# Two levels of Strassen's form for the output projections of chunk 14, with the inner sums on VectorE

## The chip, the cores and the metric

The kernel runs on one core of a Trainium2 chip. The metric is the time of one execution in device microseconds (us). TensorE (PE) multiplies, and its weight loads are shown as a row of their own (PEld); VectorE (DVE), ScalarE (ACT) and GpSimd (POOL) do elementwise work; SyncE (SP) issues most DMAs. Every engine works through its own queue in program order.

## The reference, cut to what matters

All data are float32. `x` has 8 sequences of 1024 rows of 512, so 8192 rows.

```
xn = layernorm(x)
proj = xn @ W1 + b1                       # 512 -> 3 * 1024: hidden, forget, input
...                                        # gated recurrence along each sequence -> out_h
s = out_h @ W2 + b2                       # 1024 -> 512
shared = (silu(xn @ sgate) * (xn @ sup)) @ sdown        # 512 -> 1024 -> 512
routed = expert e of each row (the best of 32 by xn @ gate_w), the same form with its own weights
x = x + s * silu(shared + routed)
```

The change is in the two products with a 1024 x 512 matrix: `out_h @ W2` (called half 0 in the kernel) and the shared expert's product with `sdown` (half 1).

## The kernel before, in words

**Two stages.** In the first stage the rows are taken in 16 chunks of 512 (`NCHUNK`, `T`), numbered 0 to 15. Each chunk has its projections in (W1, sgate, sup: 20 jobs), its recurrence, and its projections out. In the second stage the 32 experts work on rows gathered by expert; its order doesn't depend on the change. A last loop for overflowing experts follows.

**The order of the first stage** is written out by hand: a loop over slots (`now`), 7 slots to a job, so 140 to a chunk (`SC`). In each slot every engine gets its next instructions: two TensorE products of a projection in (`multiply`, line 925), the steps planned for that slot (`at(slot, ...)`), and as many steps of the generator `project_out` as `due(slot)` says. The projections out of chunk c run while chunk c + 1 is projected in: half 0 over the first 62 slots, half 1 over the other 74. The projections out of chunk 15 have nothing beside them: they begin with slot 142 after the start of chunk 15, at a rate of 7/3 steps to a slot, and after them the expert stage begins.

**Projections out.** Each half of a chunk is 7 products (`UNIT`, Strassen's form of one level). A *whole* product is 8 matmuls with 256 columns (line 1461), evicted as one tile of 128 x 512 by ScalarE or VectorE (`out_copy`, lines 1325 and 1331). A *deep* product is split again into 7 inner products (`INNER`: P1, P2, P5, P6, P3, P7, P4) of 2 matmuls with 128 columns each (line 1407), one inner product to a step. In the profile each of these float32 matmuls leaves two records, so a whole product has 16 and a deep one 28. `deep(b)` says which products are deep: those of chunks 1 to 13. Chunks 0, 14 and 15 are whole.

The inner products of one deep product begin three steps apart and those of neighbouring products are interleaved: P1 at step 7b, P2 at 7b + 3, and so on to P4 at 7b + 18. So the last deep unit has 6 inner products left when its own steps are over; they are put between the matmuls of the next unit's first whole product, one for one (`left` in `project_out`).

P1, P6, P7 and P4 share one region of a PSUM bank: each is added onto the one before it, which must have been evicted first. P2, P3 and P7 are evicted by VectorE, which adds a part kept from before (line 1416), P1, P5, P6 and P4 by `out_copy`. So P4 waits for VectorE's eviction of P7, three steps ahead of it.

A deep product needs 4 sums of blocks of its left operand (`inner_sum`, line 1389): 8 instructions of 128 x 128 where the operand is a block of the activations themselves (products P1, P2, P4 of `UNIT`), else 4 of 128 x 256. GpSimd makes them. Each sum has one buffer (`i1` to `i4`).

**Weights for the projections out** come by `out_fetch` on SP's queue into a ring of 3 tiles of 512 KB: a whole product's weights by one DMA of 512 KB (`w_whole`), the weights of four inner products by four of 128 KB (`w_pieces`). A fetch is issued when the tile three back is used up. After the slot loop three more tiles (`far`) are added.

**Beside chunk 15's projections in**, GpSimd writes the table of the rows' places with 64 small indirect DMAs (line 1706, `tab`). SP reads it back (`two`), VectorE merges it, and the first expert's rows are gathered by it.

Of the kernel before, what the change touches and what calls it, by code (L numbers as in the profile page):

```python
# [34 lines left out]
def tile_kernel(  # L35
# [45 lines left out]
    nc = tc.nc  # L81
# [8 lines left out]
    NCHUNK = N // T  # L90
# [436 lines left out]
    def alloc2(shape, tag, name):  # L527
# [11 lines left out]
            lambda t, b, e=e: pools["fours"][:, b, e * CT + t : e * CT + t + 1],  # L539
# [606 lines left out]
    ALL = [(c, half, name) for c, half in units for name in UNIT]  # L1146

    def deep(b):
        return 0 < ALL[b][0] < NCHUNK - 2

    LAST = max(b for b in range(len(ALL)) if deep(b))
    inner_of = {}
    for b in range(len(ALL)):
        if deep(b):
            for i, name in enumerate(INNER):
                inner_of[7 * b + 3 * i] = (b, name)
# [4 lines left out]
    def out_order():  # L1161

        piece = []
        for b, u in enumerate(ALL):
            if deep(b):
                piece += [(7 * b + k) for k in range(7)]
                if b == LAST:
                    piece += [7 * b + k for k in range(7, 19)]
                continue
            yield from groups(piece)  # L1170
            piece = []
            yield ("whole", b)
            if u[0] == 0:
                yield ("made", b)
        yield from groups(piece)
# [84 lines left out]
    def out_part(c, half, p):  # L1260
        h = (rnn_h, ffn_h)[half][c, p]
        return [h[:, k, m * HALF : (m + 1) * HALF] for m in range(2) for k in range(2)]
# [102 lines left out]
    def inner_block(b, m, k):  # L1365

        c, half, name = ALL[b]
        part = slice(m * P, (m + 1) * P)
        if name in RAW:
            return [out_part(c, half, 2 * k + q)[RAW[name]][:, part] for q in range(2)]  # L1370
        return [out_s[(c, half), SUM[name]][:, 2 * k : 2 * k + 2, part]]

    def inner_sum(b, q):

        o = inner[b, q] = jp.tile([P, 2, P], FP, tag=f"i{q}", name=f"i{q}_{b}", bufs=1)
        A11, A12, A21, A22 = (inner_block(b, m, k) for m in range(2) for k in range(2))
        n = len(A11)
        parts = [o[:, i, :] for i in range(2)] if n == 2 else [o]

        def made(q):  # L1380
            t = inner[b, q]
            return [t[:, i, :] for i in range(2)] if n == 2 else [t]

        l, r, what = {
            1: lambda: (A21, A22, ALU.add), 2: lambda: (made(1), A11, ALU.subtract),
            3: lambda: (A11, A21, ALU.subtract), 4: lambda: (A12, made(2), ALU.subtract),
        }[q]()
        for o, l, r in zip(parts, l, r):
            nc.gpsimd.tensor_tensor(o, l, r, what)  # L1389

    def inner_lhs(b, name):
        if name in RAW:
# [33 lines left out]
    def project_out():  # L1426
# [11 lines left out]
        for b, (c, half, name) in enumerate(ALL):  # L1438
            if deep(b):
                for k in range(7):  # L1440
                    step(7 * b + k)
                    if k % 3 == 0 and k < 9:
                        inner_sum(b, (1, 2, 4)[k // 3])
                    if k == 2 and deep(b - 1):
                        inner_sum(b - 1, 3)
                    yield
                continue
# [4 lines left out]
            for q in range(2):  # L1452
                for p in range(NP):
# [27 lines left out]
                    if left and b > LAST:  # L1481
                        step(left[0])
                        if left[0] == 7 * LAST + 9:
                            inner_sum(LAST, 3)
                        left.pop(0)
                        yield
# [540 lines left out]
```

## Time and profile before

| what | us |
|---|---|
| runs of the kernel: median (lowest to highest of 3) | 4140.21 (4139.19 to 4141.18) |
| the profiled execution: its time | 4142.6 |
| its span, first to last instruction | 4140.9 |
| TensorE busy in the span | 4057.0 (98%) |
| VectorE, ScalarE, GpSimd busy | 2647.0, 2203.4, 2198.8 |
| chunk 13's projections in (out of chunk 12, deep) | 2206.6 to 2376.1 |
| chunk 14's projections in (out of chunk 13, deep) | 2376.1 to 2551.0 |
| chunk 15's projections in (out of chunk 14, whole) | 2551.0 to 2735.6 |
| the rest of the projections out of chunk 15 | to 2781.1 |
| the experts | from 2781.1 |

Each stretch of a chunk is cut so that it holds the 560 records that a chunk leaves at line 925. Line numbers (L925) are those of the kernel before. In a timeline a row holds the start, the time until its last instruction ends, the engine, line and operation, `out<-in` by tile names, and the count; in brackets the idle time before it and what ended it. In a table by stretches the columns are the stretch, its length, the busy time of PE, PEld, DVE, ACT and POOL with their counts, the granted TensorE clock, the share of the DMA engines and GB/s.

### The profile page before, as it was taken

Reading aid. Unit: us, or ns where it says so; the run is one execution under the profiler, and the core shown is the slowest. Engines: PE = TensorE matmul, PEld = TensorE weight load, DVE = VectorE, ACT = ScalarE, POOL = GpSimd, SP = SyncE. Lnnn points to the kernel's source line nnn. Section 1 sums busy time; section 2 is a strip of 40 time slices with the busy share of each in tenths; the row PEclk is TensorE's granted clock in tenths of the full one; section 3 lists DMA queues with packets and bytes.
Section 4 is the critical chain, followed back from the end, with each engine's and each line's share of the span. In section 5 each row is a group of like instructions: output and inputs, shape, how many; then the busy total and the mean of one; then the engine's idle time right before and its main releaser. Section 6 shows DMA issues by size and latency. Waiting matters only on the chain. (4 is left out here: it accounts for less than half of the span.)

```text
span 4140.9 us, 70159 instructions
## 1 busy us (share of the span) xinstructions
PE 4057.0 (98%) x23699; PEld 3642.7 (88%) x23699; DVE 2647.0 (64%) x4553; ACT 2203.4 (53%) x4582; POOL 2198.8 (53%) x2539
## 2 busy tenths in 40 slices
PE   8999999999999999999999999999999999999997
PEld 6788889888888888988988888887899999999997
DVE  6666676677766766667676677444556656666631
ACT  5777676776767667676677765731222222222210
POOL 4324565565655655556655564634555555565542
PEclk9999999999999999999999999999999999999999
DMA  8788787787877778778777776666777787888884
GB/s 285 254 285 270 236 257 250 249 259 244 260 242 242 252 254 255 249 236 258 253 249 251 237 250 205 187 214 200 211 228 229 223 245 230 244 254 234 247 259 117
DMA packets 731387, 994.43 MB, mean 240 GB/s; under 512 B 75468, under 2 KB 523884, under 8 KB 730772
## 3 DMA queue, kind: packets, MB, share of 16 engines
q1 hardware_dynamic: 682020, 896.52, 68.0%
q0 software_dynamic: 46880, 89.20, 8.7%
q8 instruction: 193, 3.16, 0.3%
q10 hardware_dynamic: 2128, 4.19, 0.3%
q14 instruction: 166, 1.36, 0.1%
HBM read 858.39 MB, written 149.21 MB: 243 GB/s over the span
## 5 line engine op out<-in xcount | busy, mean ns | idle before, releaser
L925 PE MATMUL b<-t,sums 128*128 128x256 f32 x2536 | 652.7, 380 | 11.0 <-ACT u L939 5.2
L339 PE MATMUL acc<-e_h,e_wd 128*128 128x284 f32 (+26 forms) x2048 | 514.7, 394 | 0.0
L925 PEld LDWEIGHTS b<-t,sums 128*128 128x128 f32 x2536 | 454.2, 191 | 61.7 <-ACT u L939 7.3
L1407 PEld LDWEIGHTS u<-w_pieces,i 128*128 128x128 f32 x2912 | 435.4, 191 | 73.2 <-POOL i L1389 31.5
L1407 PE MATMUL u<-w_pieces,i 128*128 128x128 f32 x2912 | 445.4, 275 | 22.4 <-POOL i L1389 16.1
L339 PEld LDWEIGHTS acc<-e_h,e_wd 128*128 128x128 f32 x2048 | 373.6, 190 | 64.9
L260 POOL DMA_INDIRECT e_xs<-rec,fours x276 | 301.2, 1091 | 91.3 <-issue 88.6
L925 PE MATMUL b<-t,nat 128*128 128x256 f32 x1268 | 327.2, 381 | 5.3 <-ACT u L939 3.7
L925 PE MATMUL c<-xnT,sums 128*128 128x256 f32 x1268 | 326.8, 380 | 2.8 <-ACT p L939 2.8
L925 PE MATMUL c<-t,sums 128*128 128x256 f32 x1268 | 328.0, 381 | 0.1
L925 PE MATMUL b<-xnT,nat 128*128 128x256 f32 x1268 | 327.7, 381 | 0.0
L925 PE MATMUL a<-xnT,nat 128*128 128x256 f32 x1268 | 326.0, 380 | 0.2 <-ACT c L939 0.2
L302 POOL COPY pin<-e_h 1x1 f32<-1x1 f32 x148 | 37.7, 255 | 477.1 <-DVE e_h L447 348.3
L1389 POOL TENSOR_TENSOR i<-s 128x256 f32<-128x256 f32 x208 | 222.5, 1072 | 99.5 <-PE u L1407 75.8
L941 ACT ACTIVATE u<-b,vec 128x256 f32<-128x256 f32 x378 | 180.9, 478 | 175.3 <-PE b L925 168.8
L925 PEld LDWEIGHTS b<-xnT,nat 128*128 128x128 f32 x1268 | 226.2, 191 | 35.4 <-DMA w_pieces<-d_P 6.7
L925 PEld LDWEIGHTS b<-t,nat 128*128 128x128 f32 x1268 | 227.4, 191 | 32.2 <-ACT u L939 5.0
L925 PEld LDWEIGHTS c<-xnT,sums 128*128 128x128 f32 x1268 | 226.1, 191 | 28.8 <-ACT p L939 6.0
L925 PEld LDWEIGHTS c<-t,sums 128*128 128x128 f32 x1268 | 225.6, 191 | 27.6 <-DVE lgT L694 5.3
L925 PEld LDWEIGHTS a<-xnT,nat 128*128 128x128 f32 x1268 | 226.0, 191 | 23.2 <-ACT c L939 0.6
L414 ACT COPY e_s<-e_b 128x284 f32<-128x284 f32 (+21 forms) x216 | 84.4, 391 | 239.2 <-PE e_b L405 239.2
L1407 PEld LDWEIGHTS u<-w_pieces,s 128*128 128x128 f32 x1248 | 187.6, 191 | 26.3 <-DVE o L1416 10.2
(328 smaller groups left out, 9523.5 us busy)
## 6 DMA issues: line engine op xcount, KB each, us to landing
w_pieces<-d_P SPq DMA_DIRECT2D x1274, 128.0 KB
sums<-sdram SPq DMA_DIRECT2D x300, 512.0 KB
nat<-in_L_attn_W_dram SPq DMA_DIRECT2D x192, 512.0 KB
e_w<-L_ffn_routed_gate_w_dram SPq DMA_DIRECT2D x126, 512.0 KB
e_w<-n_L_ffn_routed_up_w_dram SPq DMA_DIRECT2D x126, 512.0 KB
e_wd<-L_ffn_routed_down_w_dram SPq DMA_DIRECT2D x31, 2048.0 KB
nat<-L_ffn_shared_gate_w_dram SPq DMA_DIRECT2D x64, 512.0 KB
nat<-n_L_ffn_shared_up_w_dram SPq DMA_DIRECT2D x64, 512.0 KB
```

What stands on the lines that cost most here:

```text
L260: nc.gpsimd.indirect_dma_start(out=self.xs[t][:, b, :], out_offset=None, in_=rec1.rearrange("n (a d) -> (n a) d", a=NA), in_offset=bass.In ...
L302: nc.gpsimd.tensor_copy(pin, self.mark)
L339: nc.tensor.matmul(accs[m][:, :W], lhsT=self.wd[:, j, m * P : (m + 1) * P], rhs=h[:, :W], start=(j == 0), stop=(j == NI - 1),)
L414: nc.scalar.copy(o[:, :W], ps[:, :W])
L925: nc.tensor.matmul(ps, lhsT=lhs[:, k, :], rhs=rhs[:, k, :], start=(new and k == 0), stop=(k == KQ - 1),  skip_group_check=True,)
L941: nc.scalar.activation(o, ps, AF.Identity, bias=bias(n, block))
L1389: nc.gpsimd.tensor_tensor(o, l, r, what)
L1407: nc.tensor.matmul(ps, lhsT=lhs, rhs=w[:, i, :], start=(name == "P1" and i == 0), stop=(i == 1), skip_group_check=True,)
```

## The change

Chunk 14's 14 products become deep, and `inner_sum` uses VectorE for them. Chunks 1 to 13 keep theirs on GpSimd. Everything else follows from `deep(b)`: `PER` gives each half of chunk 14 49 steps instead of 56, the 6 inner products left over by chunk 13 go on among chunk 14's deep steps, and 6 of chunk 14's now stand among the first matmuls of chunk 15's output.

```
     def deep(b):
-        return 0 < ALL[b][0] < NCHUNK - 2
+        return 0 < ALL[b][0] < NCHUNK - 1
...
     def inner_sum(b, q):
 
         o = inner[b, q] = jp.tile([P, 2, P], FP, tag=f"i{q}", name=f"i{q}_{b}", bufs=1)
+        eng = nc.vector if ALL[b][0] == NCHUNK - 2 else nc.gpsimd
         A11, A12, A21, A22 = (inner_block(b, m, k) for m in range(2) for k in range(2))
...
         for o, l, r in zip(parts, l, r):
-            nc.gpsimd.tensor_tensor(o, l, r, what)
+            eng.tensor_tensor(o, l, r, what)
```

More of the change, by code (lines that the diff above doesn't have):

```diff
@@ L1148, in deep @@
     def deep(b):
-        return 0 < ALL[b][0] < NCHUNK - 2
+        return 0 < ALL[b][0] < NCHUNK - 1
     LAST = max(b for b in range(len(ALL)) if deep(b))
@@ L1375, in inner_sum @@
         o = inner[b, q] = jp.tile([P, 2, P], FP, tag=f"i{q}", name=f"i{q}_{b}", bufs=1)
+        eng = nc.vector if ALL[b][0] == NCHUNK - 2 else nc.gpsimd
         A11, A12, A21, A22 = (inner_block(b, m, k) for m in range(2) for k in range(2))
@@ L1388, in inner_sum @@
         for o, l, r in zip(parts, l, r):
-            nc.gpsimd.tensor_tensor(o, l, r, what)
+            eng.tensor_tensor(o, l, r, what)
     def inner_lhs(b, name):
```

## The prediction

> **What bounds the kernel now.** First the page's busy times.
>
> ```profile
> span 4140.9 us, 70159 instructions
> PE 4057.0 (98%) x23699; PEld 3642.7 (88%) x23699; DVE 2647.0 (64%) x4553; ACT 2203.4 (53%) x4582; POOL 2198.8 (53%) x2539
> ```
>
> TensorE is the bound: what counts is the time that its matmuls take in its queue, and the places where it waits. Next the stretches of a deep chunk (out of chunk 12) and of the one that changes (out of chunk 14).
>
> ```profile
> 2206.60:2376.10 169.50, 167.62 (x966) 150.15 (x966) 118.42 (x193) 118.84 (x242) 96.83 (x117) 1.00 0.78 249
> 2551.00:2735.60 184.60, 179.82 (x836) 157.65 (x835) 97.92 (x144) 116.97 (x212) 107.48 (x104) 0.99 0.59 182
> ```
>
> The second is longer, with VectorE and the DMA engines less busy. What a matmul costs, and the one long wait, stand in TensorE's timeline there.
>
> ```profile
> 2554.44 0.61 PE L1407 MATMUL u<-w_pieces,i 128*128 128x128 f32 x4
> 2554.88 1.03 PE L925 MATMUL c<-xnT,sums 128*128 128x256 f32 x4
> 2555.75 0.59 PE L1461 MATMUL u<-w_whole,h 128*128 128x256 f32 x2
> 2556.18 1.03 PE L925 MATMUL b<-xnT,nat 128*128 128x256 f32 x4
> 2560.89 0.71 PE L1407 MATMUL u<-w_pieces,s 128*128 128x128 f32 x4 [3.68 <-DVE o L1416]
> ```
>
> Read start to start: 4 records with 128 columns take 0.44 us (0.111 each; 0.1117 from (0.61 - 0.275) / 3, with the 275 ns of one), 2 with 256 columns take 0.43, 4 take 0.87 (0.216). The wait of 3.68 is for VectorE's eviction of a deep P7, before its P4. Then the place where chunk 15's projections out begin.
>
> ```profile
> 2726.34 1.03 PE L1461 MATMUL u<-w_whole,h 128*128 128x256 f32 x4
> 2727.20 1.03 PE L925 MATMUL b<-t,sums 128*128 128x256 f32 x4
> 2728.06 0.59 PE L1461 MATMUL u<-w_whole,h 128*128 128x256 f32 x2
> 2729.76 1.56 PE L1461 MATMUL u<-w_whole,h 128*128 128x256 f32 x6 [1.10 <-DVE h L1036]
> ...
> 2762.10 2.21 PE L1461 MATMUL u<-far,sh 128*128 128x256 f32 x9 [1.42 <-ACT T L1325]
> ```
>
> TensorE waits for the last recurrence of chunk 15, and later once for a bank. VectorE's timeline says why.
>
> ```profile
> 2722.68 1.23 DVE L1024 SCALAR_TENSOR_TENSOR h<-m,h 128x1024 f32<-128x1024 f32 x1 [2.94 <-ACT h L1021]
> 2723.94 1.63 DVE L1027 TENSOR_TENSOR f<-f,h 128x1024 f32<-128x1024 f32 x1
> ...
> 2726.51 0.68 DVE L1345 TENSOR_TENSOR R<-R,T 128x512 f32<-128x512 f32 x1
> 2727.22 1.29 DVE L1345 TENSOR_TENSOR o<-o,R 128x512 f32<-128x512 f32 x2
> 2728.43 1.28 DVE L1036 TENSOR_TENSOR_SCAN h<-i,carry,f 128x512 f32<-128x512 f32 x1
> ...
> 2732.61 1.20 DVE L1072 TENSOR_TENSOR sh<-ssig,u 128x1024 f32<-128x1024 f32 x1
> ```
>
> From 2722.68 to 2733.7 it never idles. Whatever stands behind these in its queue waits.
>
> **The change part by part.** *TensorE's work.* Removed: 14 whole products, 224 records x 0.216 = 48.4 us. Added: 14 deep ones, 392 x 0.1117 = 43.8. Saved: **4.6 us**, all on the bound. The leftover pieces (24 records) only move, from chunk 14's start to chunk 15's.
>
> *VectorE's work.* 48 sums of 128 x 128 and 32 of 128 x 256, 42 evictions with a sum, 12 with a bias, less 3 of 128 x 512. No row has a 128 x 128 sum out of SBUF; the nearest is L1416 (0.28 listed, 0.20 to its successor); for 128 x 256 it is L1276 (0.42 and 0.34). By the successor's start: 48 x 0.20 + 32 x 0.34 + 54 x 0.20 - 3 x 0.6 = 29.5 us. 97.9 + 29.5 = 127 in about 180, 71%; the deep chunk above has 70% and lost little, so VectorE doesn't become the bound on average. GpSimd's queue stays as it was: its sums of chunk 14 never existed. ScalarE gets 44 evictions of 0.27 less 11 of 0.59, +5 us: 68%, hidden. SP issues 98 DMAs of 128 KB (12.5 MB) for 14 of 512 KB (7.2 MB): +5 MB in 180 us, 182 to 211 GB/s where the deep chunk runs at 249. Hidden; if not, a late tile costs what a tile costs, 2 to 4 us.
>
> *Middle of the chunk.* New waits are those of deep products. The deep chunk's 169.5 us hold 560 x 0.216 + 392 x 0.1117 = 164.8 and other matmuls; what is left, about 2.5 us, bounds them above; below is 0. Most of it ended by GpSimd's sums or by the preparation of the next chunk, which chunk 15 doesn't have, so I take **+0.7**.
>
> *Start of the chunk.* The 3.68 stays: VectorE is behind with the table and the recurrence. Two inner sums of the first deep unit now stand in its queue ahead of the awaited eviction: **+0.5** (0 to 2, if the backlog that ended by 2568.5 is worked off later).
>
> *Start of chunk 15's output.* Here the change adds waits. Six inner products now alternate with the first whole matmuls: P7 and P4 of the last deep unit but one are the 2nd and 6th steps, so three steps in slots have become 0.43 x 3 + 0.45 x 2 + 0.87 = 3.06 us of TensorE's time. P4 needs P7's eviction, which VectorE's queue now holds behind both scans and L1072. The end of that block: 2733.7, less R and the two adds, which now come later (1.92), plus one inner sum and two evictions (0.9), is 2732.7, or 6.4 us after the first whole matmul (2726.34). The slots become some 2% shorter (in half 1 a job of 8.3 us has 4.6 deep steps of 0.45 for 5.3 whole ones of 0.43, 0.2 less) while ScalarE's chain ahead of L1024 gets two more evictions, so about 6.9. P4 waits 6.9 - 3.06 = 3.8 us. The last unit's P4 then stands one matmul behind its P7, and between their eviction and the one before are three adds (0.34 + 0.6 + 0.6): another 0.7. The wait for the recurrence (1.3 with the gap behind it) is hidden under this. After 3.68 us of idling the granted clock fell:
>
> ```profile
> 2560.00:2565.00 5.00, 4.12 (x14) 3.38 (x15) 5.00 (x10) 0.64 (x2) 4.40 (x5) 0.67 0.10 23
> ```
>
> Ten records from 2561.43 to 2565.28 then took 3.85 us where 2.2 were due, 1.7 more; after idling 1.10 and 1.42 nothing of it is seen. 3.8 is nearer to 3.68, so I count it, with part of it inside the last P4's wait: +1.0. Sum: 3.8 + 0.7 + 1.0 - 1.3 = **+4.2** (bounds -1.3, if VectorE is on time, and +7, if both P4s wait in full and the clock falls).
>
> The Trainium skill (TensorE: Matmul & The Clock Gate, What's Actually Happening) has the clock halve after an idle window of about 3.4 us, with a window that runs freely, so that a wait of 3.8 only may be caught. By the rule at its kindest the +1.0 is absent and the end is 1 us earlier.
>
> *The later wait for a bank* (1.42) ended with ScalarE, which was held by issuing the first expert's weights. TensorE now gets there some 4 to 6 us later against the slots, so most of it goes: **-1.0** (-1.6 to +2).
>
> Sum: -4.6 + 0.7 + 0.5 + 4.2 - 1.0 = -0.2. The experts begin where TensorE ends (first expert matmul at 2780.9), their rows landed by 2756 and ScalarE's DMA queue had moved their first weights by 2769, 12 us before, and their queues' order is unchanged, so the shift goes through to the end. The profiled execution is 4142.6, so 4142.4 on its own scale; the median of the runs is 4140.2, so **4140.0**. What is saved in the chunk is paid back at its end.
>
> **The rivals.** *The end is on time.* If VectorE reaches the eviction before TensorE does, the 4.2 become -1.3: 4140.2 - 4.6 + 0.7 + 0.5 - 1.3 - 1.0 = 4134.5. For it: 3 us of slack would do. Against: VectorE's block has no gap in it, and the eviction stands behind it.
>
> *VectorE gets behind (slower).* At the start of the chunk it is saturated from 2540 to 2568, and the deep units bring about 3 us more by 2577. If it doesn't recover, each of the next three P4s waits 2 to 3 us and the clock falls once more (1.7): +8 on the forecast, 4148. It decides if VectorE's unbroken stretch goes past about 2580, since P4 leaves it some 4 us. For it: 9.72 of 10 us busy from 2550 to 2560. Against: from 2575 on VectorE was half idle.
>
> *The saving isn't there.* If a 128-column record cost its weight load (191 ns), 392 of them would cost 75 us, +26: 4167. The four in 0.44 us rule it out, nearly.
>
> **How the numbers follow.** Forecast, 4137.5 to 4143: 0.52. End on time, whole or in part, 4133 to 4137.5: 0.28. VectorE behind, 4143 to 4151: 0.16. Others: 0.04. The range 4133.5 to 4146 leaves out about 0.05 below and 0.12 above. 0.2% is 8.3 us, about what a measurement can tell from no change: faster (under 4131.9) 0.04, slower (over 4148.5) 0.08, the same 0.88.
>
> **What would show it.** Right: 28 records to a product at 0.111; no wait for GpSimd at line 1407 in this stretch; one wait of 3 us or more for VectorE's line 1416 just after the first whole matmuls of chunk 15, where the wait for L1036 was; no wait of 1.4 for ScalarE's T. Wrong: that wait under 1 us (then 4134), or several waits for line 1416 between 2565 and 2600 (then 4148).

## The result, and the profile after

The changed kernel takes 4148.94 us (median of 18 runs, 4144.79 to 4152.2), the kernel before in the same runs 4141.23 (18 runs, 4138.12 to 4142.88): a ratio of 1.0018 [1.0011, 1.0025]. The prediction was 4140.0 with a range of 4133.5 to 4146. The time lies 3 us above that range: a small loss where no change was forecast. Line numbers of the kernel after are one higher from L1376 on (the inner sums are L1390, the evictions with a sum L1417, the inner products L1408, the whole matmuls L1462).

First the busy times on the page of the kernel after (span 4149.1 us).

```profile
PE 4056.0 (98%) x23867; PEld 3646.6 (88%) x23867; DVE 2682.1 (65%) x4684; ACT 2205.4 (53%) x4615; POOL 2195.7 (53%) x2539
```

TensorE has 168 records more, as forecast (392 for 224). Its busy time hardly moved, though the work fell; that is the first sign of time at half clock, in which the same work shows as more busy time. The table by stretches of the kernel after (stretch, length, busy PE, PEld, DVE, ACT, POOL, granted clock, DMA share, GB/s) has chunk 14's projections out, then the rest up to the experts, then four places of 5 us:

```profile
2550.90:2738.40 187.50, 175.83 (x994) 158.44 (x994) 134.25 (x278) 119.88 (x247) 112.68 (x105) 0.97 0.65 199
2738.40:2789.50 51.10, 48.24 (x222) 42.07 (x221) 21.80 (x38) 6.41 (x11) 11.02 (x14) 0.97 0.79 271
2560.00:2565.00 5.00, 1.39 (x5) 1.36 (x6) 5.00 (x11) 0.13 (x1) 4.49 (x5) 0.56 0.56 176
2565.00:2570.00 5.00, 5.00 (x23) 4.42 (x22) 3.97 (x9) 1.41 (x5) 2.92 (x3) 0.76 0.14 42
2730.00:2735.00 5.00, 4.01 (x17) 3.51 (x18) 2.82 (x6) 0.27 (x1) 2.19 (x2) 0.66 0.00 0
2765.00:2770.00 5.00, 4.54 (x13) 3.78 (x14) 4.49 (x10) 1.39 (x3) 0.00 (x0) 0.66 1.03 375
```

The first stretch is 2.9 us longer than before (184.6), the second 5.7 longer (45.4 before). The experts take the same time in both traces (1359.7 us from the first expert matmul to the end of the span, 1360.0 before), so all of it is lost ahead of them. The clock column gives the time at half clock: (1 - 0.56) x 5 x 2 = 4.4 us and (1 - 0.76) x 5 x 2 = 2.4, together 6.8; at the other two places 3.4 each. Before, this part of the kernel had one stretch of 3.4. The waits of TensorE between 2550.9 and 2789.5 (us in total, times, longest) are these:

```profile
PE u L1408 <- DVE o L1417: 9.7, 2, 5.6
PE u L1462 <- ACT o L1325: 2.9, 1, 2.9
PE u L1408 <- DVE T L1417: 1.9, 2, 1.5
```

Before they were 3.7 (start of the chunk), 1.4 (ScalarE's T) and 1.1 (L1036). The place where chunk 15's projections out begin, in TensorE's timeline after:

```profile
2725.79 0.61 PE L1408 MATMUL u<-w_pieces,i 128*128 128x128 f32 x4
2726.23 0.60 PE L1462 MATMUL u<-w_whole,h 128*128 128x256 f32 x2
2730.99 0.98 PE L1408 MATMUL u<-w_pieces,s 128*128 128x128 f32 x4 [4.16 <-DVE o L1417]
2731.76 1.06 PE L1462 MATMUL u<-w_whole,h 128*128 128x256 f32 x2
...
2735.98 0.71 PE L1408 MATMUL u<-w_pieces,s 128*128 128x128 f32 x4 [0.44 <-DVE T L1417]
```

P4 of the last deep unit but one waits 4.16, the last unit's P4 0.44, and between them the two records of a whole matmul take 1.06 us instead of 0.60: half clock. The first two rows show the price of deep records at full clock: four of them take 0.44 us from start to start, as before. VectorE's timeline after has the queue that the prediction described:

```profile
2728.34 1.27 DVE L1036 TENSOR_TENSOR_SCAN h<-i,carry,f 128x512 f32<-128x512 f32 x1
2729.54 1.19 DVE L1072 TENSOR_TENSOR sh<-ssig,u 128x1024 f32<-128x1024 f32 x1
2730.65 0.28 DVE L1417 TENSOR_TENSOR o<-u,eP 128x128 f32<-128x128 f32 x1
```

The eviction is the last row, right behind the recurrence and L1072.

**Where the 8.5 us went.** From the first record of chunk 15's projections in to the first expert matmul the traces have 229.9 us before and 238.5 after. TensorE's time there can be split by starts: each record's share of work (0.216 us with 256 columns, 0.112 with 128), gaps of over 0.35 us beyond that, and the rest.

| us | before | after | difference |
|---|---|---|---|
| work: records by their share (560 of L925 in both; 448 whole and 24 deep; 224 and 416) | 220.4 | 215.9 | -4.5 |
| long gaps | 6.7 | 15.7 | +9.0 |
| the rest (half clock and small gaps) | 1.4 | 5.4 | +4.0 |
| other matmuls | 1.4 | 1.4 | 0 |

Two of the 448 whole records are missing from the trace of before; the table counts them as there. The work is saved as forecast. What is lost is in four places: the start of the chunk (gap 3.84, now 5.72), its middle (a new 1.67 at 2650.81), chunk 15's output (1.27, now 4.32 and 0.60) and the bank (1.59, now 3.03 and 0.37). These are the profiled executions; the medians lie 7.7 us apart.

### The profile page after: what moved, and what is told of

It is laid out like the page before. It is cut to its first block, busy times and chain, and to the rows that moved or that the text cites. A ratio compares the mean times of both kernels' runs of the same rounds, so it can differ in the third digit from the quotient of the medians.

```text
span 4149.1 us, 70862 instructions
## 1 busy us (share of the span) xinstructions
PE 4056.0 (98%) x23867; PEld 3646.6 (88%) x23867; DVE 2682.1 (65%) x4684; ACT 2205.4 (53%) x4615; POOL 2195.7 (53%) x2539
## 3 DMA queue, kind: packets, MB, share of 16 engines
q14 instruction: 168, 1.38, 0.1%
## 5 line engine op out<-in xcount | busy, mean ns | idle before, releaser
L925 PE MATMUL b<-t,sums 128*128 128x256 f32 x2536 | 652.9, 380 | 10.8 <-ACT u L939 5.2
L1408 PEld LDWEIGHTS u<-w_pieces,i 128*128 128x128 f32 x3136 | 470.3, 191 | 78.4 <-POOL i L1390 31.5
L925 PEld LDWEIGHTS b<-t,sums 128*128 128x128 f32 x2536 | 452.4, 191 | 60.1 <-ACT u L939 7.2
L1408 PE MATMUL u<-w_pieces,i 128*128 128x128 f32 x3136 | 480.6, 276 | 23.9 <-POOL i L1390 16.1
L925 PE MATMUL b<-t,nat 128*128 128x256 f32 x1268 | 326.6, 380 | 6.0 <-ACT u L939 3.7
L925 PE MATMUL c<-xnT,sums 128*128 128x256 f32 x1268 | 327.0, 380 | 3.1 <-ACT p L939 3.1
L925 PE MATMUL c<-t,sums 128*128 128x256 f32 x1268 | 328.3, 381 | 0.5 <-DVE lgT L694 0.4
L925 PE MATMUL b<-xnT,nat 128*128 128x256 f32 x1268 | 327.4, 381 | 0.0
L925 PE MATMUL a<-xnT,nat 128*128 128x256 f32 x1268 | 326.0, 380 | 0.0
L1390 POOL TENSOR_TENSOR i<-s 128x256 f32<-128x256 f32 x208 | 221.3, 1066 | 99.9 <-PE u L1408 76.1
L925 PEld LDWEIGHTS b<-xnT,nat 128*128 128x128 f32 x1268 | 224.8, 191 | 34.5 <-DMA w_pieces<-d_P 7.5
L925 PEld LDWEIGHTS b<-t,nat 128*128 128x128 f32 x1268 | 226.3, 191 | 32.2 <-ACT u L939 5.0
L925 PEld LDWEIGHTS c<-xnT,sums 128*128 128x128 f32 x1268 | 225.0, 191 | 28.8 <-ACT p L939 6.8
L925 PEld LDWEIGHTS c<-t,sums 128*128 128x128 f32 x1268 | 224.3, 191 | 27.4 <-DVE lgT L694 6.2
L925 PEld LDWEIGHTS a<-xnT,nat 128*128 128x128 f32 x1268 | 224.9, 191 | 22.1 <-ACT c L939 0.3
L1408 PEld LDWEIGHTS u<-w_pieces,s 128*128 128x128 f32 x1344 | 202.3, 191 | 35.3 <-DVE o L1417 17.1
L1408 PE MATMUL u<-w_pieces,s 128*128 128x128 f32 x1344 | 206.1, 276 | 13.5 <-DVE o L1417 13.0
```

Source lines behind the costliest of these rows:

```text
L925: nc.tensor.matmul(ps, lhsT=lhs[:, k, :], rhs=rhs[:, k, :], start=(new and k == 0), stop=(k == KQ - 1),  skip_group_check=True,)
L1390: eng.tensor_tensor(o, l, r, what)
L1408: nc.tensor.matmul(ps, lhsT=lhs, rhs=w[:, i, :], start=(name == "P1" and i == 0), stop=(i == 1), skip_group_check=True,)
```

## The experiments

Theory A: the work is saved and four separate waits of TensorE, with the half clock behind three of them, take it back. Its rivals differ by run: B, VectorE's load as such; C, a gain that the edit would bring without the inner products; S and W, what stretches VectorE at the start. Each group of kernels ran beside the kernel before on one chip, and the groups on different chips, so what compares is the difference to the time of before in the same row.

| run | time | before beside it | ratio [interval] | stretch to the experts |
|---|---|---|---|---|
| after | 4148.94 | 4141.23 | 1.0018 [1.0011, 1.0025] | 238.5 |
| e1_pool_sums | 4160.30 | 4143.17 | 1.0036 [1.0023, 1.005] | 246.5 |
| e2_left_inside | 4143.14 | 4143.17 | 0.9998 [0.9989, 1.0007] | 231.1 |
| e3_late_weights | 4145.29 | 4143.17 | 1.0005 [0.9996, 1.0014] | 235.0 |
| e4_sum_later | 4144.91 | 4143.17 | 1.0005 [0.9996, 1.0014] | 232.7 |
| e5_inside_late | 4141.77 | 4141.97 | 0.9999 [0.999, 1.0008] | 229.6 |
| e6_three_edits | 4139.43 | 4141.97 | 0.9995 [0.9986, 1.0004] | 227.5 |
| e7_before_late_weights | 4141.49 | 4141.97 | 0.9997 [0.9988, 1.0006] | 228.4 |
| e8_add_later | 4137.46 | 4141.97 | 0.9989 [0.998, 0.9998] | 224.9 |
| e9_last_pool_sum | 4146.89 | 4141.24 | 1.0012 [1.0003, 1.0021] | 235.9 |
| e10_writes_later | 4147.97 | 4141.24 | 1.0017 [1.0008, 1.0026] | 234.6 |
| e11_all_edits | 4138.83 | 4141.24 | 0.9993 [0.9984, 1.0002] | 226.2 |

The last column is that of the profiled execution alone (229.9 before).

### Is it VectorE's load? The sums back on GpSimd

```
-        eng = nc.vector if ALL[b][0] == NCHUNK - 2 else nc.gpsimd
+        eng = nc.gpsimd
```

> Chunk 14 deep as in the change, but its inner sums on GpSimd like those of chunks 1 to 13. Theory A (queues): the 4.6 us of TensorE's work are saved, and the loss is waits of TensorE for what stands ahead of an awaited eviction in another engine's queue. GpSimd has 112.7 us of work in chunk 15's stretch, and one chunk's sums took it 63.7 us in chunk 13's stretch, together 176 of some 185; its sums come late and TensorE waits for GpSimd at line 1408: slower than the change, 4153 to 4175 us, while the wait at the start of chunk 15's output stays (3 us or more). Rival B (VectorE's load): the sums on VectorE are the loss, and without them the saving shows: 4136 to 4141 us.

It is 17.1 us above the kernel before, where the kernel after is 7.7. Its longest waits:

```profile
PE u L1408 <- DVE o L1417: 8.9, 2, 5.2
PE u L1408 <- POOL i L1390: 3.8, 6, 0.9
PE c L925 <- ACT p L939: 2.3, 2, 1.8
PE u L1408 <- issue: 2.3, 1, 2.3
```

GpSimd is late with six sums, and the wait at chunk 15's output (the longest of the first row, 5.2) is there without one inner sum on VectorE. So the sums on VectorE aren't what costs most, and that wait comes from the place of the leftover products. That is argued so far; the next run tests it. The start of the chunk is back at a gap of 3.79 in this trace, so there the two sums did cost.

### Chunk 15's output: the leftover products inside chunk 14

```
-                if used[0] % 4 == 0 or s == left[-1]:
+                if used[0] % 4 == 0:
                     out_fetch()
...
+                while b == LAST and left:
+                    s = left.pop(0)
+                    step(s)
+                    if s == 7 * LAST + 9:
+                        inner_sum(LAST, 3)
+                    yield
...
-    PER[LAST // 7 + 1] += len([s for s in inner_of if s >= 7 * LAST + 7])
+    PER[LAST // 7] += len([s for s in inner_of if s >= 7 * LAST + 7])
```

> As the change, but the 6 inner products left over by chunk 14 are done before chunk 15's output begins, as 6 more steps of chunk 14's second half, and not among the first whole matmuls. Theory A: the waits of 4.2 and 0.4 for VectorE after the first whole matmuls and the half clock behind them go, and the wait of about 1.1 for L1036 comes back: 4 to 6 us less, 4143 to 4145 us. Rival B: VectorE's work is the same, so is the time: 4147 to 4150 us.

The six products are done in chunk 14's second half, and the kernel is level with before. The waits of this kernel up to the experts:

```profile
PE u L1408 <- DVE o L1417: 5.5, 1, 5.5
PE u L1408 <- DVE T L1417: 3.2, 2, 2.1
PE u L1468 <- ACT T L1325: 1.8, 1, 1.8
```

The 4.16 is gone, and rival B with it. The gain on the kernel after is 7.7 us, more than the 4 to 6 expected: the bank's wait has shrunk too (third row), with no half clock behind it. The second row holds the middle of the chunk (2.1) and one of 1.1 at 2724.85; the start stays at 5.5.

### The bank: the first expert's weights later

After TensorE's wait for a bank ended with ScalarE, so ScalarE's queue in the kernel after is the next view.

```profile
2762.66 1.02 ACTq L209 DMA_DIRECT2D e_w<-L_ffn_routed_gate_w_dram  x2
...
2764.82 0.59 ACT L1325 COPY o<-u 128x512 f32<-128x512 f32 x1 [15.41 <-DVE fours L1743]
```

The ACTq rows are ScalarE's own DMA issues: they stand ahead of the eviction for which TensorE waits, and ScalarE had evicted nothing for 15.4 us before it. SP's queue of the same kernel:

```profile
2752.64 9.81 SPq L1742 DMA_DIRECT2D number<-table  x8
```

SP's eight issues of the reads of the table end at 2762.45, 0.2 us before ScalarE's DMAs start. Before, four and four of them stood around a fetch of `w_whole`; they ended at 2757.91:

```profile
2747.31 2.30 SPq L1741 DMA_DIRECT2D number<-table  x4
2751.31 6.60 SPq L1741 DMA_DIRECT2D number<-table  x4
```

ScalarE's issue started right behind:

```profile
2757.98 2.10 ACTq L209 DMA_DIRECT2D e_w<-L_ffn_routed_gate_w_dram  x2
```

The two go together in all seven kernels that issue these weights at `k = 6`: SP's last read ends between 2757.1 and 2774.5, and ScalarE's first issue follows within 0.35 us (in one, it comes 0.04 before that end). This doesn't show that one holds the other up; both could wait for the same thing. The experiment leaves SP alone and puts ScalarE's issue ten steps later:

```
-        if k in (6, 22):
+        if k in (16, 22):
```

> As the change, but ScalarE issues the first expert's first weights 10 slots later (k = 16 for 6), behind its evictions. Theory A: the wait of 2.9 us for a bank at 2765 and the half clock behind it go: 3 to 5 us less, 4144 to 4146 us, and the experts don't begin later for want of weights. Rival B: no change, 4147 to 4150 us.

In ScalarE's timeline of this kernel the eviction that was at 2764.82 is nine microseconds earlier:

```profile
2755.80 0.59 ACT L1325 COPY o<-u 128x512 f32<-128x512 f32 x1 [6.32 <-PE u L1462]
...
2764.05 1.02 ACTq L209 DMA_DIRECT2D e_w<-L_ffn_routed_gate_w_dram  x2
```

The bank's wait is gone, a gap of 1.20 at 2774.07 comes in its place, and the kernel is 2.1 us above before instead of 7.7 (in the profiled stretch the gain is 3.5). The same edit on the kernel before is the control:

> The kernel before with one edit: the DMA of the first expert's weights is issued by ScalarE ten steps later. Control for the bank's wait. Theory A: before's own wait of 1.42 us (gap 1.69) goes and at most 1.3 comes in its place near 2774: 0 to 1.7 us under before. Rival C (the edit gains by itself some 4 to 6 us, whatever the inner products do, as it did on the kernel after): 4 to 6 us under before.

It gains 0.5 us (1.5 in the profiled stretch), so C falls: of the 5.6 us that the edit brings on the kernel after, all but about 0.5 are a loss that the change had caused.

### The start of the chunk: the awaited eviction ahead of the sums

```
-                    if k % 3 == 0 and k < 9:
+                    if k % 3 == 0 and k < 9 and (b, k) != (14 * (NCHUNK - 2), 0):
                         inner_sum(b, (1, 2, 4)[k // 3])
+                    if (b, k) == (14 * (NCHUNK - 2), 1):
+                        inner_sum(b, 1)
```

> As the change, but the first inner sum of chunk 14's first product is given to VectorE one step later, behind the eviction that TensorE waits for at the start of the chunk. Theory A: the two sums took 2.3 us ahead of that eviction, so the wait of 5.6 shrinks to 3.5 to 4, with a shorter half clock: 2 to 3 us less, 4146 to 4147 us. Rival B: VectorE has as much to do, so no change: 4148 to 4150 us.

The gap at the start is 3.53 (3.84 before, 5.72 after), with 3.4 us at half clock instead of 6.8. The time fell by more than expected, to 1.7 us above before: the bank's gap is 1.15 here, with no half clock behind it. So the bank's wait depends on when TensorE gets there, and the terms aren't independent.

Why had two sums of 0.28 us each cost 2 us? VectorE in the kernel after:

```profile
2560.49 0.68 DVE L837 TENSOR_TENSOR t<-xnT 128x512 f32<-128x512 f32 x1
2561.09 2.26 DVE L1390 TENSOR_TENSOR i<-h,h 128x128 f32<-128x128 f32 x2
2563.28 0.28 DVE L1417 TENSOR_TENSOR o<-u,eP 128x128 f32<-128x128 f32 x1
```

Two such sums elsewhere take 0.48. GpSimd at that time:

```profile
2559.66 1.89 POOL L1707 DMA_INDIRECT tab<-tok,cell  x1 [0.17 <-issue]
2561.58 0.73 POOL L951 TENSOR_TENSOR u<-u,p 128x256 f32<-128x256 f32 x1
2562.26 0.73 POOL L1390 TENSOR_TENSOR i<-s 128x256 f32<-128x256 f32 x1
```

Before, the same happened 0.5 us earlier, but there VectorE's instruction at that moment was a sum of a projection in (`f<-a,p`, L951), 2.00 us long and one place behind the awaited eviction, where it cost TensorE nothing:

```profile
2560.75 2.00 DVE L951 TENSOR_TENSOR f<-a,p 128x256 f32<-128x256 f32 x1
```

Two causes can be told apart: GpSimd's sums (S) or its table write (W). One run takes away one of the sums, the other moves the writes. The edit of the first gives VectorE all four inner sums of chunk 13's last product, but three of them are done by 2551; only the last lies in this place.

```
-        eng = nc.vector if ALL[b][0] == NCHUNK - 2 else nc.gpsimd
+        eng = nc.vector if b >= 14 * (NCHUNK - 2) - 1 else nc.gpsimd
```

> The kernel after with one edit: the last inner sum of chunk 13 (128x256, L1390), that GpSimd makes at 2562.3 just as VectorE's first two sums of chunk 14 take 2.26 us, is made by VectorE, behind the awaited eviction. Theory S (VectorE's sums are stretched by GpSimd's two sums beside them, 0.73 us each): the two sums take 1.4 to 1.7 us and TensorE's gap at the start of the chunk falls from 5.7 to 4.8 to 5.2. Theory W (they are held by GpSimd's table write at 2559.7, which stays): 2.0 to 2.3 us, the gap stays at 5.5 to 5.8. In either case the time is 0 to 2 us under that of the kernel after (7.7 over before).

VectorE's two sums in this kernel:

```profile
2560.57 1.58 DVE L1390 TENSOR_TENSOR i<-h,h 128x128 f32<-128x128 f32 x2
2562.07 0.28 DVE L1417 TENSOR_TENSOR o<-u,eP 128x128 f32<-128x128 f32 x1
```

and GpSimd beside them:

```profile
2559.13 1.89 POOL L1707 DMA_INDIRECT tab<-tok,cell  x1 [0.17 <-issue]
2561.06 0.73 POOL L951 TENSOR_TENSOR u<-u,p 128x256 f32<-128x256 f32 x1
```

With GpSimd's second sum of 0.73 gone and its write (1.89) still there, they are 0.68 shorter, and the gap is 5.21. That is what S forecast. It isn't all: one sum of 0.73 explains 0.7 of the 1.1 us that the pair still takes over 0.48, and in both kernels the first VectorE sum begins 0.49 us before GpSimd's first sum, beside the write alone, and isn't done by then (of the pair, the first takes 2.06 in the kernel after and 1.38 in this run, the second 0.28 in both).

```
-            at(first + (21 * i) // 10, d.enter, i)
+            at(first + max(4, (21 * i) // 10), d.enter, i)
```

> The kernel after with one edit: GpSimd's first two table writes (L1707) start up to four steps later, in the slot of the third, so that none lies beside the first two inner sums of chunk 14. Theory W (a table write holds VectorE's sum): the two sums fall from 2.26 to between 0.5 and 1.0 us, the gap at the start of the chunk to 3.9 to 4.5, the time by 3 to 5 us against the kernel after. Theory S (GpSimd's sums hold it): they now come about 1.9 us earlier and stretch what stands before the sums on VectorE (L1072 or L837) instead, so the gap stays over 5.2 and the time within 1.5 us of the kernel after.

GpSimd's sums come earlier, and VectorE's timeline shows two stretched rows:

```profile
2560.09 1.21 DVE L837 TENSOR_TENSOR t<-xnT 128x512 f32<-128x512 f32 x1
2561.22 1.01 DVE L1390 TENSOR_TENSOR i<-h,h 128x128 f32<-128x128 f32 x2
```

L837 has grown by 0.53 and the sums by as much; GpSimd's two sums took 1.70 and 1.17 instead of 0.73 each. The gap is 4.99, between the two forecasts, so this run alone decides nothing. With the one before it, the traces support S for the larger part, 0.7 us for each GpSimd sum: the engines hold each other up, and which of the two pays depends on which came first. The 0.4 us that are left point to the write as well, which no run here separates. The Trainium skill (SBUF — State Buffer, SBUF: two separate sides) says that VectorE and GpSimd share a pair of ports as an exclusive lock, held for a whole instruction, also by a VectorE operation with two SBUF inputs against a GpSimd operation that reads SBUF. These rows agree with it: one GpSimd sum of 0.73 us fewer made VectorE's pair 0.68 us shorter. They don't settle the part beside the write.

### The edits together

> Two edits to the kernel after: the six leftover inner products of chunk 14 are done inside its second half, and the DMA of the first expert's weights is issued by ScalarE ten steps later. Theory A (the loss is four separate waits of TensorE, two of which these edits remove): beside the kernel before of the same call, 4.6 us of TensorE work saved, about 3.5 more at the start of the chunk (5.7 us gap for 3.84 and a second window at half clock), 2 more in its middle, 1.3 less at chunk 15's output (the wait for L1036), 1.7 less at the bank: 2 us under before, 0 to 4. Rival B (VectorE's load is the bound: a wait taken away at one place comes back at the next): level with before or up to 3 us above it, with a new wait of 2 us or more for VectorE behind 2725.

Level with before (-0.2), at the edge of what A gave. The new wait that B wanted behind 2725 isn't there; the longest gap of this kind is 1.30 at 2723.98.

> As the run before it, and the first inner sum of the chunk's first deep product stands one step later, behind the awaited eviction. Theory A: the start of the chunk is back at a gap of 3.5 to 3.9 us with one window at half clock, so 6 us under before (4 to 8). Rival B: within 2 us of before; the sums taken from the start come up as a longer wait for VectorE's L1417 later in the chunk.

2.5 us under before, where A had 6, and its interval holds 1. The waits of this kernel:

```profile
PE u L1408 <- DVE o L1417: 3.4, 1, 3.4
PE u L1408 <- DVE T L1417: 3.2, 2, 2.1
PE u L1470 <- ACT o L1325: 0.7, 1, 0.7
```

The start is back at 3.4 as A says. The expectation took off the 1.1 for L1036 and the 1.4 for the bank in full, but a wait of 1.1 for L1417 (in the second row) and one of 0.7 came in their places. By the ledger: work -4.5, long gaps 8.0 for 6.7, the rest 2.2 for 1.4, in all -2.4.

What was left is the middle. There P7's eviction stands on VectorE behind the recurrence, L1072 and two adds of 128 x 512 (L1345), as VectorE's timeline of the same kernel has it:

```profile
2645.53 1.75 DVE L1036 TENSOR_TENSOR_SCAN h<-i,carry,f 128x512 f32<-128x512 f32 x1
...
2648.65 0.68 DVE L1345 TENSOR_TENSOR o<-o,o 128x512 f32<-128x512 f32 x1
2649.36 0.69 DVE L1345 TENSOR_TENSOR o<-o,R 128x512 f32<-128x512 f32 x1
2649.97 0.28 DVE L1417 TENSOR_TENSOR T<-u,eP 128x128 f32<-128x128 f32 x1
```

The next run moves these adds four steps back:

```
-            at(now + 2, out_add, b)
+            at(now + (6 if b == 14 * (NCHUNK - 2) + 5 else 2), out_add, b)
```

> As the run with three edits, and the two 128x512 adds (L1345) of chunk 14's first P3 stand four steps later, behind the eviction of the next product's P7. Theory A: the wait in the middle of the chunk (1.5 to 2.3 us) goes or falls under 0.7, so 1 to 2 us under the run with three edits, 7 us under before. Rival B: the wait stays within 0.4 us, since the recurrence and not the adds holds VectorE, and the time is that of the run with three edits.

Its waits for `T`, where the run with three edits had 3.2:

```profile
PE u L1408 <- DVE T L1417: 1.9, 2, 1.1
```

The middle's gap falls from 2.26 to 0.93, so what stands ahead of the adds (the recurrence and L1072) holds 0.9 of it and the adds the rest. The time is 2.0 us under the run with three edits and 4.5 under before, where A had 7; the ratio is 0.9989 [0.998, 0.9998]. This version beats both kernels by little: the interval just leaves out 1, and it is the best of the eleven kernels with edits.

> The four edits that gave 4137.46 (4.5 under before) and the table writes later. The awaited eviction already stands ahead of the first sums here, so neither theory sees a stretch in front of it: the gap at the start stays at 3.3 to 3.7 and the time within 1.5 us of 4.5 under before. If the start's gap falls under 2.5 or the time by over 2 us more, GpSimd's writes hold something earlier in VectorE's queue, which neither theory has.

With the writes later too, the gap at the start grows to 4.06, since L837 ahead of the eviction is stretched to 1.21 as in the run with the writes later alone. The time is 2.4 under before. Neither expected figure was met; S explains the gap, and the time misses the margin by 0.6, where the intervals of the two runs overlap.

## Why the prediction was wrong, point by point

**TensorE's work**, forecast -4.6: -4.5. Right, at 0.112 and 0.216 a record.

**VectorE's load**, forecast 127 us in the chunk: 134.25, 7 us more. The forecast priced the sums at their undisturbed rows: the 48 small ones took 17.0 us where 0.28 each gives 13.4, the 32 large ones 15.2 where 0.41 each gives 13.1. It was still not the bound: the rival "VectorE gets behind" wanted waits of 2 to 3 us for line 1416 between 2565 and 2600, and there is none. The time lies in the range that the prediction gave to this rival, but not for the rival's reason. DMA ran at 199 GB/s where 211 was forecast, and hid. "The saving isn't there" is out.

**Chunk 15's output**, forecast +4.2 from 3.8, 0.7, 1.0 and -1.3. Measured: 4.32 and 0.60 for gaps, 1.7 for 3.4 us at half clock, -1.27: about +5.3. Every part was there, the half clock at 1.7 for 1.0 and the others at nearly their price; the experiment that moved the leftovers confirms it. So the rival "The end is on time" failed, as argued.

**The later wait for a bank**, forecast -1.0, is the step that failed most: +1.4 for the gap (and 0.4 behind it, partly in what follows), then 1.7 at half clock, about +3. The sign "no wait of 1.4 for ScalarE's T" came true in name alone: the wait is 2.9 and for another tile. The prediction reasoned that TensorE arrives later and so finds ScalarE done. But ScalarE was held by its own DMA issue, which comes with the end of SP's table reads, and that end moved too, by 4.5 us (2757.91 to 2762.45). The bounds (-1.6 to +2) were too near as well, since they left out the clock. The experiment shows that the place of ScalarE's issue makes the wait; that SP's reads are what the issue waits for, and SP's order what makes them end late, is read from timelines and not tested.

**The start of the chunk**, forecast +0.5 (0 to 2), is the second: +1.9 for the gap and 0.2 for the half clock, since TensorE then worked at half clock for 3.8 us instead of 3.4. The two sums were right, the price was not: 2.26 us for 0.4, for the larger part because of GpSimd's sums beside them. The trace of before had that row, `f<-a,p` with 2.00 us behind the eviction, and the prediction did not ask what makes it long.

**The middle**, forecast +0.7 with an upper bound of 2.5: +1.7 in one wait. That it would be a wait of a deep product was right, the size low; the prediction named no place for it, and expected most of such waits to end with GpSimd or the next chunk's preparation. It ended with VectorE's eviction of a P7.

**The sum**: -4.5 + 5.3 + 3 + 2.1 + 1.7 = 7.6 of the 8.5; the rest lies in small gaps. The two largest misses, the bank and the start, were not independent: where the start's wait was cut, the bank's shrank with it. By the forecast's own terms the errors all had one sign: each place where VectorE, ScalarE or GpSimd queue for each other cost more than its nearest row. **Passing through to the end** was right: the experts kept their 1360 us.

**The clock rule.** The prediction set a price of 1.0 beside a rule of the Trainium skill (TensorE: Matmul & The Clock Gate, What's Actually Happening) by which a wait of 3.8 us may be caught only by chance. Waits of 2.9 and 4.2 in the kernel after each had 3.4 us at half clock behind them, one of 5.6 had 6.8. In the run with the sums on GpSimd one of 2.3 sufficed, while waits of 2.1 in the runs with one, two and three edits had none. The length of the wait doesn't decide this alone. A wait of 2.1 us near 250, which all thirteen traces have, was followed by half clock in eight of them and not in the other five; one of 2.8 us near 68, in seven and not in six. What decides, in these traces, is where the wait falls. The stretches at half clock begin on a grid of 3.41 us that runs through each trace (in the kernel after they begin at 2560.62, 2731.29 and 2765.42, which is 50 and 10 steps apart). Cut on that grid, the wait near 250 looks like this in the kernel before:

```profile
247.50:250.91 3.41, 1.32 (x9) 0.83 (x12) 2.71 (x5) 2.76 (x7) 0.83 (x1) 1.00 0.69 200
250.91:254.32 3.41, 3.41 (x12) 1.51 (x5) 3.41 (x6) 2.10 (x4) 0.19 (x1) 0.50 1.00 306
```

and in the kernel after:

```profile
246.38:249.79 3.41, 2.45 (x11) 1.63 (x9) 0.48 (x2) 3.41 (x8) 0.00 (x0) 1.00 0.49 166
249.79:253.21 3.42, 2.29 (x13) 1.07 (x14) 3.39 (x5) 1.71 (x4) 1.03 (x1) 1.00 0.93 273
253.21:256.62 3.41, 3.41 (x17) 3.00 (x17) 3.41 (x9) 3.16 (x7) 0.00 (x0) 1.00 1.07 364
```

Before, the wait lies whole in one step, in which TensorE idles 2.09 us, and the next step is at half clock. After, a boundary splits it into 0.96 and 1.12, and the clock stays. Over all thirteen traces, from 30 to 4100 us, every step at full clock with 1.96 us or more of idle time was followed by half clock, and none with 1.94 or less. By this, as an estimate, a wait of more than twice 1.95 us is always caught, and one between 1.95 and 3.9 only if it falls so. So the half clock that the prediction counted behind a wait of 3.8 us was all but certain, and the one behind the bank's 2.9 is in part bad luck. That the grid runs freely agrees with the page; an idle step doesn't have to be idle as a whole.

## What to carry to other kernels

When work is taken from the bounding engine, list the places where another engine's queue already ends last, and price the new instructions in that queue by what runs beside them there, not by their row elsewhere. An instruction put ahead of an awaited one costs its stretched time on the path; here the same instruction one place later cost nothing. A wait that is expected to vanish because the bound arrives later has to be checked against what its releaser waits for: that may have moved with it.

## What the runs showed of the hardware

- Two VectorE sums of 128 x 128 took 2.26 us beside the end of a table write and two GpSimd sums, 1.58 beside the end of such a write and one sum, 0.48 at most other places.
- Eight issues of reads of a small table took 9.81 us of SP's queue, and ScalarE evicted nothing for 15.4 us around its own DMA issue.
- TensorE's half clock came in steps of 3.41 us on a fixed grid: after each step at full clock with 1.96 us or more of idle time, and after none with 1.94 or less (thirteen traces).
